# Four stage borders of a transformer, spectral and scan kernel: where SBUF tiles lie and when first loads are queued

## Chip, cores and metric

One Trainium2 chip, one of its cores. The metric is device time in microseconds of one execution; lower is better. The kernel has five instruction streams that matter here: PE (matmul), VectorE (DVE), ScalarE (ACT), GpSimd (POOL) and SyncE (SP), which issues nearly all DMAs. Each stream runs its instructions in order.

## What is computed

The input is one image of 48 x 48 tokens with 768 channels, in f32. Four layers follow one another:

```
# layer 0: transformer block, 12 heads of 64
qkv  = layernorm(x) @ qkv_w + qkv_b
attn = softmax(q @ k.T * scale + rel_h[...] + rel_w[...])     # 2304 x 2304 per head
x    = x + (attn @ v) @ proj_w + proj_b
x    = x + gelu(layernorm(x) @ w1 + b1) @ w2 + b2             # 768 -> 3072 -> 768
# layers 1 and 3: spectral mixing
xs   = rfft2(x)                                               # complex, over the 48 x 48 grid
o1   = relu(block_diag(xs, w1) + b1); o2 = block_diag(o1, w2) + b2   # 8 blocks of 96, complex
x    = irfft2(softshrink(o2, 0.01)) + x
# layer 2: twelve steps of a 3 x 3 depthwise diffusion with gates, then silu(H @ W_out + b_out)
```

## The kernel before

The kernel is one straight program; its stages come one after the other and meet at five borders.

**Queries, keys, values** (`qkv_phase`). Tokens are handled in three superblocks `sb` of 768. For each, matmuls make q, k, v (dense products run as seven products of half blocks instead of eight; the sums of weight blocks that this needs are made once and stored). Beside them run 24 "position steps" per superblock: 12 of `rel_h` and 12 of `rel_w` (L400). A step loads a table `relD` of 192 KB (L378, four buffers), runs four matmuls, and its result is split by ACT and VectorE into three bf16 parts (L370 to L373), which go to DRAM as `rh_d` and `rw_d` (L389). `advance()` (L433) issues loads until three steps are ready, then runs one step. At the end of the last superblock 16 steps are left. A bound on the scores is computed (L460 to L477), four steps run (L478), the work pools are closed, `ahead(1)` (L481, `load_ahead`, L1283) opens the attention's tiles and issues nine loads for its first chunk (one of queries, L516; eight of biases, L495 and L496), and then the remaining twelve `rel_w` steps run.

**Attention.** A branch on the bound picks `attention_bounded` (the one that runs here) or `attention_any`. 36 chunks (6 pairs of heads x 6 query blocks of 384) have six work items each; in an item PE runs `products` (L556), `scores` (L564) and the `values` of the item before (L585). Beside it POOL makes the block sums of the projection and MLP weights (`weight_sums`), the projection's into `ps_d`.

**Projection** (`proj_phase`). After the branch, all seven blocks of `ps_d` are loaded (L714), 576 KB each. `block_sums` adds parts of oT on VectorE (L136 to L139). Blocks n=0 and n=1 use oT itself as left operand, n=2 the first sum. A block is nine matmuls, which the trace lists as 18 entries.

**MLP** (`mlp_phase`). Twelve hidden tiles per half (`ml_h`), weights in four slots (`ml_w`), seven products of the second layer per superblock (`product`, L911); each product has twelve steps f of three matmuls, six entries in the trace. Between them `follow` (L1507) takes the first transform of the next layer along: a call runs the rows loaded by the call before (L1353, result stored to `yu`, L1355), and loads the next input from `xa_d` (L1499), the MLP's stored output. In the very last product the calls are at f=3 and f=9:

```
                    if f in ((3, 9) if (sb, n) == (NTB // 2 - 1, 6) else (6,)):
                        follow(psum)
```

The last block of half 0 comes after the MLP, in steps 1 and 4 of the mix.

**First spectral layer** (`afno_first`, `spectrum_mix`). Per item (40 of them, in 44 pipelined steps): f_x (L1412), block products (L1426 to L1428, L1447, L1448), f_u (L1462); input tiles `yt` are read from `yu` (L1385), four items each, and results `us` stored back (L1469). Then the rows are gathered again (`gt`, L1483) for the last transform f_w (L1549), whose result is x2T, the scan's input. The same mix runs for layer 3 (`afno_second`), where f_w (L1580) is followed by an addition on VectorE (L1582) and the output's DMAs.

**Scan** (`scan_phase`). Its input projection is L1076, its twelve steps L1166, its output L1228 and L1237.

**What sets the order and the waits.** SBUF pools are stacks, one from the left and one from the right. A pool waits until all tiles of the pools whose place it takes are done with. The order of the instructions of an engine is made by the framework's scheduler: first in code goes first, but where an instruction's inputs are not ready yet by the scheduler's own reckoning, a later one that is ready goes ahead. [...]

The places that matter at the border from MLP to spectrum, in bytes per partition: ml_c (constants, x2nT and sums) 17,056 to 52,544; ml_x 52,544 to 71,716; ml_w 71,744 to 96,320; x1 (rows of `follow`) 96,320 to 121,344; ml_h 129,504 to 229,344. Over them: f1_g (gathers and rows) 17,056 to 48,608; f1_c (spectral weights, o1) 48,608 to 76,512; f1_y (yt, us) 76,512 to 114,912; f1_s 114,912 to 134,112. So f1_c and f1_y reach into ml_w.

Of the kernel before, what the change touches and what calls it, by code (L numbers as in the profile page):

```python
# [11 lines left out]
F32 = mybir.dt.float32  # L12
# [7 lines left out]
P = 128  # L20
G = 48
T = G * G
# [6 lines left out]
TB = 384  # L29
NTB = T // TB  # L30
# [6 lines left out]
NB, BS = 8, 96  # L37
# [142 lines left out]
def qkv_phase(tc, ident, x, qkv_w, qkv_b, relT, rel_d, ln_g, ln_b, q_d, k_d, v_d, rw_d, rh_d, wqk_d, wv_d, flag, home, ahead):  # L180
# [18 lines left out]
    with (  # L199
# [163 lines left out]
        with tc.tile_pool(name="qkv_o", bufs=1, side="right") as op:  # L363
# [114 lines left out]
            for _ in range(4):  # L478
                advance()
            inner.close()  # L480
            ahead(1)  # L481
            while steps or ready:
                advance()
# [36 lines left out]
    return keys_values, chunk  # L520


def attention_bounded(tc, ahead, oT, beside):

# [14 lines left out]
    with (  # L539
# [64 lines left out]
        for i in range(len(work) + 1):  # L604
            if i % 7 == 3:
                next(other, None)
            if i < len(work):
                c, k0 = work[i]
                pr, qc = c
                if k0 == 0:  # L610
                    nxt = (pr, qc + 1) if qc + 1 < T // QB else (pr + 1, 0)
                    if nxt[0] < NC:
                        load_chunk(qbs[nxt[1] % 2], nxt)
                    if qc == 1 and pr + 1 < NC:
                        load_keys_values(kvs[(pr + 1) % 2], pr + 1)
# [13 lines left out]
            pass  # L629


def attention_any(tc, ident, oneh, q_d, k_d, v_d, rw_d, rh_d, oT, beside):


    nc = tc.nc
# [2 lines left out]
    with tc.tile_pool(name="an_o", bufs=2) as op:  # L638
        for _ in beside(op, lambda name: op.tile([P, 2, TB], F32, tag="p", name=name)):
            pass  # L640
    with (
        tc.tile_pool(name="an_c", bufs=1) as cp,
        tc.tile_pool(name="an_h", bufs=1) as hp,
# [11 lines left out]
        for h in range(NH):  # L655
# [5 lines left out]
            for i in range(NTB):  # L661
                load_bias(nc, bt[:, :, :, i * TB : (i + 1) * TB], rw_d, rh_d, h, i)
            for t in range(NT):
                s = sp.tile([P, T], F32, tag="s", name=f"an_s_{h}_{t}")
# [12 lines left out]
                nc.scalar.activation(s, s, AF.Exp, bias=nm)  # L677
                if t % GQ == 0:
                    pT = pp.tile([P, NT, GQ * P], F32, tag="pT", name=f"an_pT_{h}_{t}")
                col = (t % GQ) * P  # L680
                for k0 in range(0, NT, 4):
                    n = min(4, NT - k0)
                    ps = ps_t.tile([P, 512], F32, tag="t", name=f"an_pt_{h}_{t}_{k0}")
                    for j in range(n):
                        k = k0 + j
                        nc.tensor.transpose(ps[:, j * P : (j + 1) * P], s[:, k * P : (k + 1) * P], ident)
                    ev(pT[:, k0 : k0 + n, col : col + P], ps[:, : n * P].rearrange("p (k q) -> p k q", q=P))
                if t % GQ == GQ - 1:
# [12 lines left out]


def proj_phase(tc, x, ps_d, proj_b, oT, xr_d):

    nc = tc.nc
    with (
# [2 lines left out]
        tc.tile_pool(name="pj_x", bufs=1, side="right") as xp,  # L709
        tc.tile_pool(name="pj_p", bufs=6, space=PSUM) as pm,  # L710
    ):
        w = wp.tile([P, 7, NC2, TB], F32, tag="w", name="pj_wt")
        for n in range(7):
            nc.sync.dma_start(w[:, n], ps_d[:, n])  # L714
        pb = load_bcast(nc, wp, proj_b, C, "pj_b")
        for sb in range(NTB // 2):
            rows = lambda n: slice((2 * sb + n) * TB, (2 * sb + n + 1) * TB)
# [11 lines left out]
                nc.gpsimd.tensor_tensor(o, o, added[half, n], ALU.add)  # L729
                nc.sync.dma_start(xr_d[rows(n), cols(half)].rearrange("(t p) c -> p t c", p=P), o)  # L730

            rows_in_seven(nc, pm, f"pj_{sb}", rhs, lambda n: w[:, n], xp, emit)


def weight_sums(nc, pool, gate, pw, w1, w2, ps_d, w1s_d, w2s_d):
# [51 lines left out]
def mlp_phase(tc, ident, w1s_d, b1, w2, w2s_d, b2, ln_g, ln_b, xr_d, xa_d, follow_in):  # L787
# [8 lines left out]
    with (  # L796
# [91 lines left out]
        def second_layer(sb):  # L888
# [22 lines left out]
            def product(n, left, right):  # L911

                ps = [pm.tile([P, 512], F32, tag="m", name=f"p2_{sb}_{n}_{t}") for t in range(3)]
                for f in range(NF2):
# [12 lines left out]
                        V.tensor_tensor(hs[1, f], hs[1, f], hs[2, f], ALU.subtract)  # L927
                        V.tensor_tensor(hs[0, f], hs[3, f], hs[2, f], ALU.subtract)

                    if f in ((3, 9) if (sb, n) == (NTB // 2 - 1, 6) else (6,)):  # L930
                        follow(psum)
                return [p[:, :TB] for p in ps]

# [323 lines left out]
def block_kernel(ctx: ExitStack, tc: tile.TileContext, a: dict):  # L1257
# [48 lines left out]
    w2s_d = dram.tile([4, P, NF2, TB], F32, tag="w2s_d", name="w2s_d")  # L1306
    ps_d = dram.tile([P, 7, NC2, TB], F32, tag="ps_d", name="ps_d")
    beside = lambda pool, gate: weight_sums(nc, pool, gate, a["proj_w"], a["mlp_w1"], a["mlp_w2"], ps_d, w1s_d, w2s_d)
    bounded = nc.values_load(flag)
    with tc.If(bounded > 0) as which:  # L1310
        attention_bounded(tc, ahead, oT, beside)
    with which.Else():
        attention_any(tc, ident, oneh, q_d, k_d, v_d, rw_d, rh_d, oT, beside)
    at_stack.close()
    xr_d = dram.tile([T, C], F32, tag="xr_d", name="xr_d")
    proj_phase(tc, x, ps_d, a["proj_b"], oT, xr_d)
    oT_close()
    xa_d = dram.tile([NTB, TB, C], F32, tag="xa_d", name="xa_d")
    yu = [dram.tile([YR, G // 2, TB], F32, tag=f"yu{i}", name=f"yu{i}") for i in range(2)]
# [6 lines left out]
    nc.sync.dma_start(wsc, a["W_scan"].rearrange("(c p) n -> p c n", p=P))  # L1326
    afno_first(tc, a, yu, x2T, follow_in)

    closes = []

# [27 lines left out]
def spectrum_mix(tc, name, a, layer, yu, psum, keep, side, halves, beside):  # L1358
# [9 lines left out]
    HB = NB // 2  # L1368
    with (
        tc.tile_pool(name=f"{name}_c", bufs=1, side=side) as cp,  # L1370
        tc.tile_pool(name=f"{name}_y", bufs=2, side=side) as yp,
        tc.tile_pool(name=f"{name}_s", bufs=2, side=side) as sp,
    ):
        fh = cp.tile([BS, BS], F32, tag="fh", name=f"{name}_fh")
# [6 lines left out]
        ys = {}  # L1381

        def load(half, kc):
            yt = yp.tile([BS, KC, TB], F32, tag="yt", name=f"{name}_yt_{half}_{kc}", bufs=3)
            nc.sync.dma_start(yt, yu[half][4 * KC * kc : 4 * KC * (kc + 1)].rearrange("(k q) p c -> (q p) k c", q=4))  # L1385
            us = yp.tile([BS, KC, TB], F32, tag="us", name=f"{name}_us_{half}_{kc}")
            ys[half, kc] = yt, us

        nc.sync.dma_start(w1t, w1)
# [6 lines left out]

        o1s = []
        for i in range(3):
            o1 = cp.tile([BS + 1, KC, 3, G], F32, tag=f"o1{i}", name=f"{name}_o1{i}")
            nc.vector.memset(o1[BS : BS + 1, :, :, :], 0.0)  # L1400
            nc.vector.memset(o1[BS : BS + 1, :, 1, :], 1.0)
            o1s.append(o1)
# [75 lines left out]
            beside(step)  # L1478


def load_spectrum(nc, pool, yu, half, g, name):
    gt = pool.tile([YR, 4, TB], F32, tag="gt", name=f"{name}_gt_{half}_{g}", bufs=3)
    nc.sync.dma_start(gt, yu[half][:, 4 * g : 4 * g + 4, :])  # L1483
    return gt

# [32 lines left out]
    return follow  # L1518


def afno_first(tc, a, yu, x2T, follow_in):

# [6 lines left out]
    x2v = x2T.rearrange("p c (h w) -> p c h w", w=HD)  # L1529
    nc.gpsimd.memset(x2v[:, :, :, G:], 0.0)  # L1530
    with (
        tc.tile_pool(name="f1_g", bufs=1, side="left") as gp,
        tc.tile_pool(name="f1_p", bufs=8, space=PSUM) as pm,
    ):

# [2 lines left out]

        iw = gp.tile([4 * KW, BS], F32, tag="iw", name="f1_iw")
        follow = follow_in(gp, 1)  # L1540
        spectrum_mix(tc, "f1", a, "L1", yu, psum, True, "left", (1, 0), lambda step: follow(psum) if step in (1, 4) else None)
        nc.sync.dma_start(iw, a["iw"])
        for half in (1, 0):
            for g in range(NTB):
                gt = load_spectrum(nc, gp, yu, half, g, "f1")
# [7 lines left out]
def afno_second(tc, a, x3, yu):  # L1553
# [4 lines left out]
    with (  # L1558
# [15 lines left out]
        for half in range(2):  # L1574
            cols = slice(half * TB, (half + 1) * TB)
            for g in range(NTB):
                gt = load_spectrum(nc, gp, yu, half, g, "f3")
                for i in range(4):
                    ps = psum(f"w_{half}_{g}_{i}")
                    nc.tensor.matmul(ps[:BS, :TB], lhsT=iw, rhs=gt[: 4 * KW, i, :], start=True, stop=True)  # L1580
# [118 lines left out]
```

## Time and profile before

| | |
|---|---|
| three timed runs | 3902.34, 3902.94, 3906.36 us (median 3902.94) |
| the profiled execution | 3896.0 us |
| its span, first to last instruction | 3893.8 us |
| PE busy | 3755.5 us, 96% |
| VectorE, ACT, POOL busy | 53%, 29%, 17% |
| mean granted PE clock | 0.977 |
| bytes moved | 460.43 MB, mean 118 GB/s |
| chain that ended last | PE 87%, DVE 5%, DMA 4% |

The stages on the span's clock, by their first matmuls: queries, keys and values to 480, the last position steps to 510, attention 513.5 to 1690.1, projection from 1701.2, MLP from about 1838 to 2854.2, first mix from 2872.5, f_w from about 3070, scan projection from 3133.7, scan from 3296.8, second mix 3655.3 to 3849.1, last stage to the end.

How to read it: a row of the time order gives start, length, engine, source line, operation and tiles, a count, and in brackets the idle time before it with what ended it. A row of the waits gives who waited for what, the sum, how many times and the longest. "SPq" is the queue of DMA issues, where a length covers a run of several. A row of the windows gives the busy time of PE, PE's weight loads, DVE, ACT and POOL with counts, then the granted PE clock, the DMA engines' busy share and GB/s.

### The profile page before, as it was taken

The page shows a single profiled execution, that of the slowest core. Times are in us where ns is not written, and L with a number is a line of the kernel's source. Part 1 is how long each engine was busy: PE and PEld are TensorE (multiplying, and loading weights), DVE is VectorE, ACT ScalarE, POOL GpSimd, SP SyncE. Part 2 cuts the span into 40 slices and gives each one's busy share as a digit, 9 for nine tenths or more (in the row PEclk, how much of TensorE's full clock was granted, in tenths as well). Part 3 has the DMA queues.
Part 4 walks back from the last instruction along what each step waited for, and adds up shares of the span by engine and source line. Part 5 has one row for each costly group of instructions (what it writes and reads, how often), then busy time and mean ns, then how long its engine had stood idle before and what let it go on. Part 6 is the DMA issues. An engine that isn't in the chain of part 4 may idle for free.

```text
span 3893.8 us, 54463 instructions
## 1 busy us (share of the span) xinstructions
PE 3755.5 (96%) x22018; PEld 2283.2 (59%) x22018; DVE 2050.0 (53%) x3185; ACT 1141.6 (29%) x1907; POOL 654.2 (17%) x496
## 2 busy tenths in 40 slices
PE   8999989999999999989999999999979998999998
PEld 4666544444444444445555555555558876996685
DVE  6655456666666666545425233232335358995445
ACT  1322244444444444411310120021013246223341
POOL 3101011111111111024000000000023210981131
PEclk9999999999999999999999999999989789999999
DMA  7656563424232322134335434533443312110434
GB/s 256 212 186 199 177 182 95 132 88 131 96 98 89 98 89 73 30 114 161 118 106 161 151 102 123 155 111 109 142 116 98 95 36 96 35 37 23 145 98 167
DMA packets 266954, 460.43 MB, mean 118 GB/s; under 512 B 33005, under 2 KB 219365, under 8 KB 260327
## 3 DMA queue, kind: packets, MB, share of 16 engines
q1 hardware_dynamic: 257063, 436.23, 36.4%
q10 hardware_dynamic: 9632, 20.65, 1.4%
q8 instruction: 175, 2.87, 0.3%
q14 instruction: 84, 0.69, 0.1%
HBM read 318.49 MB, written 138.31 MB: 117 GB/s over the span
## 4 chain that ended last, share of the span: by engine, by line
PE 87%; DVE 5%; DMA 4%; ACT 2%; issue 1%; SPq 1%; POOL 1%; ACTq 0%; DVEq 0%; POOLq 0%
PE p L860 13%; PE p L923 13%; PE s L556 11%; PE av L585 11%; PE qk L294 6%; PE s L564 6%; PE c L1076 4%; PE v L163 3%; PE pj L163 2%; PE f_z L1447 2%; PE f_z L1448 2%; PE f_x L1412 2%; PE f_u L1462 2%; PE so L1237 2%; PE f_w L1549 2%; DVE s L1186 2%
## 5 line engine op out<-in xcount | busy, mean ns | idle before, releaser
L574 DVE TENSOR_TENSOR acc<-acc,p 128x768 f32<-128x768 f32 x576 | 581.8, 1010 | 354.1 <-ACT p L566 315.9
L566 ACT ACTIVATE p<-s 128x768 f32<-128x768 f32 x648 | 478.4, 811 | 688.7 <-PE s L564 578.9
L923 PE MATMUL p<-w,h 128*128 128x384 f32 x1512 | 492.7, 486 | 0.0
L556 PE MATMUL s<-qt,kv 64*128 64x384 f32 x2592 | 477.7, 501 | 8.4 <-ACT p L566 4.7
L585 PE MATMUL av<-p,kv 128*64 128x384 f32 x2592 | 464.5, 493 | 0.0
L923 PEld LDWEIGHTS p<-w,h 128*128 128x128 f32 x1512 | 286.3, 190 | 196.7
L556 PEld LDWEIGHTS s<-qt,kv 64*128 64x128 f32 x2592 | 232.7, 186 | 248.8 <-ACT p L566 113.8
L585 PEld LDWEIGHTS av<-p,kv 128*64 128x64 f32 x2592 | 170.0, 136 | 225.2 <-issue 215.9
L860 PE MATMUL p<-x2nT,w 128*128 128x384 f32 x864 | 293.2, 489 | 3.9 <-POOL rr L899 3.9
L294 PE MATMUL qk<-xnT,wqk 128*128 128x384 f32 x756 | 251.5, 489 | 5.6 <-DMA wqk<-wqk_d 5.6
L1166 PE MATMUL c<-H,bands 128*48 128x96 f32 x5632 | 242.1, 247 | 11.7 <-issue 11.5
L564 PE MATMUL s<-bt,oneh 120*128 120x384 bf16 x1296 | 248.8, 328 | 0.0
L1166 PEld LDWEIGHTS c<-H,bands 128*48 128x48 f32 x5632 | 234.1, 123 | 19.8 <-issue 11.9
L860 PEld LDWEIGHTS p<-x2nT,w 128*128 128x128 f32 x864 | 165.2, 191 | 119.4 <-POOL rr L899 4.1
L860 PE MATMUL p<-xT,w 128*128 128x384 f32 x648 | 220.8, 486 | 0.0
L564 PEld LDWEIGHTS <-oneh 120*128 120x128 bf16 x1296 | 109.3, 98 | 174.5 <-issue 115.4
L294 PEld LDWEIGHTS qk<-xnT,wqk 128*128 128x128 f32 x756 | 144.2, 192 | 99.7 <-issue 7.9
L899 POOL TENSOR_TENSOR rr<-rr,ml_b 128x1152 f32<-128x1152 f32 x12 | 32.1, 2675 | 955.0 <-DMA rr<-xr_d 861.6
L855 ACT ACTIVATE h<-h,ml_b 128x384 f32<-128x384 f32 x144 | 88.3, 614 | 345.9 <-DVE h L875 174.3
L1174 POOL TENSOR_TENSOR t<-s,c 128x768 f32<-128x768 f32 x80 | 144.7, 1835 | 171.9 <-DVE s L1136 160.8
L860 PEld LDWEIGHTS p<-xT,w 128*128 128x128 f32 x648 | 123.2, 190 | 85.8
L1076 PE MATMUL c<-wsc,x2T 128*112 128x357 f32 (+1 forms) x576 | 151.6, 426 | 2.0 <-DVE c L1037 2.0
(312 smaller groups left out, 4763.5 us busy)
## 6 DMA issues: line engine op xcount, KB each, us to landing
w<-w1s_d SPq DMA_DIRECT2D x36, 768.0 KB
w<-w2s_d SPq DMA_DIRECT2D x36, 768.0 KB
bt<-rh_d SPq DMA_DIRECT2D x144, 162.0 KB
w<-w1s_d SPq DMA_DIRECT2D x36, 576.0 KB
w<-in_mlp_w_dram SPq DMA_DIRECT2D x27, 768.0 KB
wqk<-wqk_d SPq DMA_DIRECT2D x12, 1344.0 KB
yu<-f_ys SPq DMA_DIRECT2D x24, 672.0 KB
f_gt<-yu SPq DMA_DIRECT2D x24, 672.0 KB
```

The lines of the kernel that those rows point to most:

```text
L163: nc.tensor.matmul(p[:, :TB], lhsT=rhs[n][:, c, t * P : (t + 1) * P], rhs=w[:, c, :], start=c == 0, stop=c == NC2 - 1)
L294: nc.tensor.matmul(p[:, :TB], lhsT=w[:, n, c, :], rhs=ops[sb][n][:, c, :], start=c == 0, stop=c == NC2 - 1)
L556: nc.tensor.matmul(ps[:, s, :QB], lhsT=keys[pr % 2][rows, kt * P : (kt + 1) * P], rhs=qbs[qc % 2][0][rows], start=True, stop=False)
L564: nc.tensor.matmul(ps[:, s, :QB], lhsT=oneh[:NBR, b % 3, :], rhs=qbs[qc % 2][1][:NBR, s, b // 3, j, :], start=False, stop=True)
L566: nc.scalar.activation(p, ps[:, :, :QB], AF.Exp)
L574: nc.vector.tensor_tensor(probs[c], probs[c], p, ALU.add)
L585: nc.tensor.matmul(avs[c][rows, :QB], lhsT=vals[pr % 2][:, kt, rows], rhs=p[:, s, :], start=kt == 0, stop=kt == NT - 1)
L860: nc.tensor.matmul(p[:, :TB], lhsT=w[n][:, c, :], rhs=rhs[n][:, c, :], start=c == 0, stop=c == NC2 - 1)
L923: nc.tensor.matmul(ps[t][:, :TB], lhsT=hs[left, f][:, t * P : (t + 1) * P], rhs=wt[:, f % KW2, :], start=f == 0, stop=f == NF2 - 1)
L1076: nc.tensor.matmul(ps[:K, i, :n], lhsT=xT[:, cc, tok : tok + K], rhs=w[:, cc, c0 : c0 + n], start=cc == 0, stop=cc == NC - 1)
L1166: nc.tensor.matmul(ps[r0 : r0 + G, k // 4, cols], lhsT=bands[:, n - GC, i, :] if gr else bands0[:, n, i, :], rhs=H[:, n, :, d : d + NPR], ...
L1174: GP.tensor_tensor(t, sc[:, ch], c1[:, m0 : m0 + GC].unsqueeze(2).to_broadcast([P, GC, RR, NPR]), ALU.mult)
```

## The change

The diff has five parts.

1. Five more position steps are issued before `ahead(1)`, so ahead of the first chunk's loads in code.
2. A tile `pw` for the first two of the seven projection blocks is allocated beside oT, and loaded by one DMA inside both branches of the attention (eight items before the end in the one that runs). `proj_phase` loads five blocks. In `attention_any` one buffer less is used, to make room.
3. The spectral pools are laid out anew. f1_g goes to the right side; the three o1 tiles and `us` go from f_c and f_y to f_s. By the sizes in the code the first mix's pools then lie at 17,056 to 36,320 (f1_c), 36,320 to 59,360 (f1_y), 59,360 to 102,560 (f1_s) and 109,344 to 140,896 (f1_g, below x2T and wsc). The calls of `follow` in the last product go from f=3 and 9 to 2 and 6.
4. The scan's weights wsc are loaded at step 8 of the first mix instead of ahead of it.
5. In the last stage `gt` has four buffers instead of three. In layer 3, f3_c, f3_y and f3_s then lie at 54,752 to 74,016, to 97,056 and to 140,256.

```diff
@@ qkv_phase
             for _ in range(4):
                 advance()
             inner.close()
+            for _ in range(5):
+                advance()
             ahead(1)
@@ attention_bounded (and attention_any: load_next() after the weight sums, s with bufs=1)
             if i % 7 == 3:
                 next(other, None)
+            if i == len(work) - 8:
+                load_next()
@@ proj_phase(tc, x, pw, ps_d, proj_b, oT, xr_d)
-        w = wp.tile([P, 7, NC2, TB], F32, tag="w", name="pj_wt")
-        for n in range(7):
-            nc.sync.dma_start(w[:, n], ps_d[:, n])
+        w = wp.tile([P, 5, NC2, TB], F32, tag="w", name="pj_wt")
+        for n in range(5):
+            nc.sync.dma_start(w[:, n], ps_d[:, 2 + n])
-            rows_in_seven(nc, pm, f"pj_{sb}", rhs, lambda n: w[:, n], xp, emit)
+            rows_in_seven(nc, pm, f"pj_{sb}", rhs, lambda n: w[:, n - 2] if n > 1 else pw[:, n], xp, emit)
@@ mlp_phase, product
-                    if f in ((3, 9) if (sb, n) == (NTB // 2 - 1, 6) else (6,)):
+                    if f in ((2, 6) if (sb, n) == (NTB // 2 - 1, 6) else (6,)):
@@ block_kernel
+    pw, pw_close = opened("pw", [P, 2, NC2, TB], "right")
+    load_pw = lambda: nc.sync.dma_start(pw, ps_d[:, :2])
-    proj_phase(tc, x, ps_d, a["proj_b"], oT, xr_d)
+    proj_phase(tc, x, pw, ps_d, a["proj_b"], oT, xr_d)
+    pw_close()
-    nc.sync.dma_start(wsc, a["W_scan"].rearrange("(c p) n -> p c n", p=P))
-    afno_first(tc, a, yu, x2T, follow_in)
+    afno_first(tc, a, yu, x2T, follow_in, lambda: nc.sync.dma_start(wsc, a["W_scan"].rearrange("(c p) n -> p c n", p=P)))
@@ spectrum_mix
-        tc.tile_pool(name=f"{name}_y", bufs=2, side=side) as yp,
+        tc.tile_pool(name=f"{name}_y", bufs=3, side=side) as yp,
-            yt = yp.tile([BS, KC, TB], F32, tag="yt", name=f"{name}_yt_{half}_{kc}", bufs=3)
+            yt = yp.tile([BS, KC, TB], F32, tag="yt", name=f"{name}_yt_{half}_{kc}")
-            us = yp.tile([BS, KC, TB], F32, tag="us", name=f"{name}_us_{half}_{kc}")
+            us = sp.tile([BS, KC, TB], F32, tag="us", name=f"{name}_us_{half}_{kc}")
-            o1 = cp.tile([BS + 1, KC, 3, G], F32, tag=f"o1{i}", name=f"{name}_o1{i}")
+            o1 = sp.tile([BS + 1, KC, 3, G], F32, tag=f"o1{i}", name=f"{name}_o1{i}", bufs=1)
@@ load_spectrum: gt with bufs=bufs; 3 in afno_first, 4 in afno_second
@@ afno_first
-        tc.tile_pool(name="f1_g", bufs=1, side="left") as gp,
+        tc.tile_pool(name="f1_g", bufs=1, side="right") as gp,
-        spectrum_mix(tc, "f1", a, "L1", yu, psum, True, "left", (1, 0), lambda step: follow(psum) if step in (1, 4) else None)
+        spectrum_mix(tc, "f1", a, "L1", yu, psum, True, "left", (1, 0), lambda step: follow(psum) if step in (1, 4) else load_next() if step == 8 else None)
```

More of the change, by code (lines that the diff above doesn't have):

```diff
@@ L520, in attention_loads, with attention_bounded @@
     return keys_values, chunk
-def attention_bounded(tc, ahead, oT, beside):
+def attention_bounded(tc, ahead, oT, beside, load_next):
     nc = tc.nc
@@ L629, in attention_bounded, with attention_any @@
             pass
-def attention_any(tc, ident, oneh, q_d, k_d, v_d, rw_d, rh_d, oT, beside):
+def attention_any(tc, ident, oneh, q_d, k_d, v_d, rw_d, rh_d, oT, beside, load_next):
     nc = tc.nc
@@ L640, in attention_any @@
             pass
+    load_next()
     with (
@@ L663, in attention_any @@
             for t in range(NT):
-                s = sp.tile([P, T], F32, tag="s", name=f"an_s_{h}_{t}")
+                s = sp.tile([P, T], F32, tag="s", name=f"an_s_{h}_{t}", bufs=1)
                 m6 = sp.tile([P, T // TB], F32, tag="m6", name=f"an_m_{h}_{t}")
@@ L700, in attention_any, with proj_phase @@
                     nc.vector.tensor_tensor(oT[r0 : r0 + HD, h // 2, g * n : (g + 1) * n], avs, bc[:HD, :n], ALU.mult)
-def proj_phase(tc, x, ps_d, proj_b, oT, xr_d):
+def proj_phase(tc, x, pw, ps_d, proj_b, oT, xr_d):
     nc = tc.nc
@@ L1308, in block_kernel @@
     beside = lambda pool, gate: weight_sums(nc, pool, gate, a["proj_w"], a["mlp_w1"], a["mlp_w2"], ps_d, w1s_d, w2s_d)
+    pw, pw_close = opened("pw", [P, 2, NC2, TB], "right")
+    load_pw = lambda: nc.sync.dma_start(pw, ps_d[:, :2])
     bounded = nc.values_load(flag)
     with tc.If(bounded > 0) as which:
-        attention_bounded(tc, ahead, oT, beside)
+        attention_bounded(tc, ahead, oT, beside, load_pw)
     with which.Else():
-        attention_any(tc, ident, oneh, q_d, k_d, v_d, rw_d, rh_d, oT, beside)
+        attention_any(tc, ident, oneh, q_d, k_d, v_d, rw_d, rh_d, oT, beside, load_pw)
     at_stack.close()
     xr_d = dram.tile([T, C], F32, tag="xr_d", name="xr_d")
-    proj_phase(tc, x, ps_d, a["proj_b"], oT, xr_d)
+    proj_phase(tc, x, pw, ps_d, a["proj_b"], oT, xr_d)
+    pw_close()
     oT_close()
@@ L1478, in spectrum_mix, with load_spectrum @@
             beside(step)
-def load_spectrum(nc, pool, yu, half, g, name):
-    gt = pool.tile([YR, 4, TB], F32, tag="gt", name=f"{name}_gt_{half}_{g}", bufs=3)
+def load_spectrum(nc, pool, yu, half, g, name, bufs):
+    gt = pool.tile([YR, 4, TB], F32, tag="gt", name=f"{name}_gt_{half}_{g}", bufs=bufs)
     nc.sync.dma_start(gt, yu[half][:, 4 * g : 4 * g + 4, :])
@@ L1518, in afno_follow, with afno_first @@
     return follow
-def afno_first(tc, a, yu, x2T, follow_in):
+def afno_first(tc, a, yu, x2T, follow_in, load_next):
     nc = tc.nc
@@ L1544, in afno_first @@
             for g in range(NTB):
-                gt = load_spectrum(nc, gp, yu, half, g, "f1")
+                gt = load_spectrum(nc, gp, yu, half, g, "f1", 3)
                 for ct in range(NC // 2):
@@ L1576, in afno_second @@
             for g in range(NTB):
-                gt = load_spectrum(nc, gp, yu, half, g, "f3")
+                gt = load_spectrum(nc, gp, yu, half, g, "f3", 4)
                 for i in range(4):
```

## The prediction

> **What bounds the kernel now.** I read the page first: PE is busy 96% of the span and carries 87% of the chain that ended last, so only time in which PE stands still, or runs at a lower clock, can be won. The list of PE's waits over the whole span says where it stands still (columns: sum in us, times, longest):
>
> ```profile
> PE f_x L1412 <- DMA f_yt<-yu: 18.2, 1, 18.2
> PE pj L163 <- DMA pj_wt<-ps_d: 11.2, 1, 11.2
> PE rw L400 <- DMA relD_w<-in_relD_dram: 11.0, 3, 9.7
> PE f_w L1580 <- DMA f_gt<-yu: 5.2, 5, 1.3
> ```
>
> All entries of the list together are some 130 us; these four, 46 us, are at the places that the diff touches, and all four wait for a DMA. The largest of the others (first LayerNorm 17.7, start of the scan 11.5) are not touched. Next I read SP's queue and PE's work at each of the four. Before the attention, SP's queue in order of time:
>
> ```profile
> 484.28 1.74 SPq L378 DMA_DIRECT2D relD_w<-in_relD_dram  x2
> 486.80 0.33 SPq L516 DMA_DIRECT2D qt<-q_d  x1
> ...
> 492.28 1.21 SPq L389 DMA_DIRECT2D rh_d<-rh  x2
> 493.53 2.28 SPq L496 DMA_DIRECT2D bt<-rh_d  x1
> 495.91 10.47 SPq L378 DMA_DIRECT2D relD_w<-in_relD_dram  x10
> ```
>
> The last ten position tables stand behind the first queries and biases (L516, L495, L496). At the spectrum, PE, then SP (two answers):
>
> ```profile
> 2850.85 3.39 PE L923 MATMUL p<-w,h 128*128 128x384 f32 x10
> 2872.47 1.89 PE L1412 MATMUL f_x<-f_fh,f_yt 96*96 96x96 f32 x10 [18.23 <-DMA f_yt<-yu]
> ```
> ```profile
> 2837.30 14.69 SPq L1355 DMA_DIRECT2D yu<-f_ys  x2
> 2854.27 0.32 SPq L1375 DMA_DIRECT2D f_fh<-in_fh_dram  x1
> ...
> 2860.86 0.39 SPq L1326 DMA_DIRECT2D wsc<-in_W_scan_dram  x1
> ...
> 2862.10 0.43 SPq L1385 DMA_DIRECT2D f_yt<-yu  x1
> ```
>
> The MLP's last product ends at 2854.24 and the next load goes at 2854.27: the spectral pools wait for a place of the MLP's weights. fh, w1, w2 and the 1839 KB of wsc then go ahead of yt, which lands at 2872.4. And after the attention PE's last `av` ends at 1690.08:
>
> ```profile
> 1688.62 1.46 PE L585 MATMUL av<-p,kv 128*64 128x384 f32 x6
> 1701.24 14.07 PE L163 MATMUL pj<-pj_wt,oT 128*128 128x384 f32 x36 [11.16 <-DMA pj_wt<-ps_d]
> ```
>
> **1. Position tables before the first queries.** Nothing is added; five table loads (L378) get priority over nine loads of the first chunk on SP. The queue isn't in code order (iw, coded after the mix, went at 2816.8), so they will interleave. Today PE runs two `rw` steps by 489.83, waits 9.70, and ends the twelfth at 509.86; VectorE ends the last split at 514.5 (L373), having had nothing from 494.0 to 501.64. Its pace is 1.12 us a step (rest_w starts 509.43, 510.55, 511.67). With tables always there it would go on at 494.0: 10 x 1.12 + 0.6 = 11.8, end 506, gain 8.4. The DMA engines don't allow quite that: they are 0.6 to 0.97 busy from 486 to 500, and the bytes (10 tables of 192 KB, chunk 1.3 MB, rh store 0.9 MB) at some 230 GB/s take 18 us from 486.8, so 505, and VectorE ends near 507.5: gain 7. If the biases still slip in front, 0. I take 6. Late next: the first chunk's biases, issued perhaps 6 us later, landing near 502 to 505, when the attention starts near 507.5; if all nine went after the five tables (5 x 1.1 us) they would land near 507 to 510 and take back up to 3. Below zero is excluded short of that, since the same DMAs are issued.
>
> **2. First two blocks of projection weights inside the attention.** One DMA more on SP in the attention (1152 KB), two fewer of 576 KB after it. The attention's SP has slack (the last chunk's loads go by 1621, and its first use is six items of 5.3 us before 1690, at 1658) and its DMA slices are 0.1 to 0.4 busy, so I cost it at nothing; without that cover, some 4 us. After the attention PE needs pw (there), oT of the last chunk (L600, ends 1692.07), and its own jump over the other branch. No row shows PE's jump alone; VectorE's is near: L600 ends at 1692.07 and L136 starts at 1695.55, with its inputs long there: 3.48 us. [...] by the row it starts at 1690.08 + 3.5 = 1693.6 and gains 7.6. I take the row, and 0.4 more for the clock: PEclk is 0.5 until about 1706 today, which costs 2.4 us, and a gap of 3.64 us before the attention still cost 1.6 (12 `s` matmuls took 3.29 instead of 2.21, and so on). So 8, from 6 to 10. Next late: block n=2, issued at about 1695.0 and landed some 6 us later, as today's first; PE needs it after 12.3 us (36 x 0.3225, plus the clock), near 1706. Its left operand (L138) ends at 1699.6. Covered by 5 us.
>
> **3. Spectral tiles over places that are free.** The constants' pool now lies at 17,056 to 36,320 bytes, over ml_c only; yt at 36,320 to 59,360, over ml_c and ml_x. Their last reader is POOL's L899 near 2815 (fw and iw, under such places, went at 2816.4 and 2816.8). So fh, w1, w2, ih and POOL's w1s, w1d (1.80 us each) go into product 5, where POOL is idle, behind nobody that PE needs before 2845 (the weights of product 6). Then yt waits for yu alone. The last rows move from f=9 to f=6: 3 x 6 x 0.3225 = 5.8 us, so the store goes at 2851.66 - 5.8 = 2845.9; the store before it (2837.30) had left the DMA engines by 2840.5, so 2849. Its input (L1499, 2830.30) was down by 2836, the row is due at 2841.6. A yt of 720 KB then takes 4 to 5 us (f_x, 576 KB, took about 5): 2853.5. VectorE empties the last banks at 2855.1 (the store of the last block goes at 2855.11). So PE starts at 2855.2 instead of 2872.47: 17.3. The start-up from the first f_x to the first f_u took 17.5 today at half clock; the same stretch in the second mix, after a gap of 1.87, took 3670.81 - 3655.34 = 15.5: another 2.0. Against it: POOL's memset of x2T (L1530, 3.9 us) waits for the last MLP store (landed 2860.8) and can stand before an Xs or an o1 sign: 0 to 1, I take 0.8. Sum 18.5. [...] But the second mix fell to half after gaps of 1.4 to 1.9, so I take the row. wsc moves behind yt; it is needed at 3133. f1's gather buffers on the other side delay the scan's bias loads until 3131.7; they need 3 to 4 us and VectorE needs them 6 us later. Nothing. The other attention branch doesn't run.
>
> **4. Fourth gather buffer in the last stage.** From 3855 to 3890 the DMA share is at its top:
>
> ```profile
> 3865.00:3870.00 5.00, 4.03 (x13) 1.84 (x13) 3.20 (x7) 0.00 (x0) 0.00 (x0) 1.00 1.06 390
> 3875.00:3880.00 5.00, 3.74 (x12) 1.79 (x12) 2.84 (x6) 0.00 (x0) 0.00 (x0) 1.00 1.04 377
> ```
>
> So the stage is bound by bytes (last two columns: DMA share, GB/s) and not by PE's 5.2 us of waits. One gather of 672 KB moves to about 3765, where DMAs are idle: 0.69 MB / 380 GB/s = 1.8 us, from 0 to 2.5.
>
> **Sum.** 6 + 8 + 18.5 + 1.8 = 34.3, some 34. The profiled execution took 3896.0 (span 3893.8 and 2.2 around it), so its like would be 3862. The median of the three timed runs, 3902.94, lies 6.9 higher; from it 3902.9 - 34 = 3869. The terms' bounds give 21 to 41, that is 3862 to 3882.
>
> **Rivals.**
> *The spectral wait changes hands* (chance 0.17). fw now lies over the MLP's hidden tiles and waits for the last store, 2860.8. If SP's order has it, or that store, before yt, yt goes at 2861 and lands at 2865.5; or the memset comes before the first Xs, which then ends near 2865.4. Either way part 3 gives 9 instead of 18.5: 3878. For it: SP and POOL are in order, and today's POOL had the memset before Xs. Against: yt and Xs are ready some us before the store is down.
> *The first queries become what is late* (0.07): part 1 gives 2 or 3, 3872.
> *The waits are not removed* (0.03): the scheduler puts the loads where they were; 3895 to 3903.
> *Slower* (0.03): the clock. In f_w (3071 to 3139) PE is 10.00 busy of 10 us at PEclk 0.50, so steady work of small matmuls doesn't always bring the clock back. If the first mix, now entered with short gaps, stayed at half, a step of 4.57 us would take about 1.9 times that (z pairs start 0.32 apart at half, 0.17 at full): 4.1 us lost a step, so from 11 of the 44 steps on the whole gain and the bound of 8 us are gone; 20 steps give 3951. Against: both mixes recovered within 27 us.
>
> **Numbers.** The likeliest case has 0.70. 0.2% (8 us) is about what a measurement of this kernel can tell from no change. Faster 0.94, within 0.03, slower 0.03. The range goes from the bound of the likeliest, with 2 us for the spread of the runs, to the far side of the first rival: 3860 to 3886.
>
> **What would show it.** Part 1: PE's wait for relD_w below 3, the first `s` near 507, no wait of `s` for bt. Part 2: PE's gap after the last `av` 2 to 4 us, the next wait of pj for pj_wt none. Part 3: fh and w1 issued near 2817 (in the old time), yt before the last xa_d store, the gap at f_x under 2. Part 4: four gathers near 3765, the last stage 1 to 2 us shorter. It is wrong if f_x still waits 8 or more, or if the scan, the attention or f_w change in length.

## The result and the profile after

| | before | after |
|---|---|---|
| median of the timed runs, us | 3903.28 | 3877.39 |
| range of the timed runs | 3902.34 to 3906.36 (4) | 3876.30 to 3878.67 (4) |
| ratio after/before | | 0.9932, 95% interval 0.9915 to 0.9950 |
| profiled execution, us | 3896.0 | 3878.45 |
| span of the profile, us | 3893.8 | 3876.6 |
| mean granted PE clock | 0.977 | 0.978 |

The medians differ by 25.9 us, the two profiled executions by only 17.5. Which of the two the change is worth is a question of its own; the experiment b_again answers it. The forecast was a gain of 34. Single executions of one kernel spread with the granted clock: of 36 of the kernel before, three took 3880 to 3883 us at a mean clock of 0.981 or 0.982, the others 3896 to 3910 at 0.972 to 0.977.

The parts are numbered here as in the prediction: the loading of the scan's weights (4 in the list of the change) counts with part 3, and part 4 is the fourth gather buffer.

First the list of PE's waits of the changed kernel (columns: sum in us, times, longest):

```profile
PE f_o L1434 <- POOL f_Xs L1424: 9.2, 4, 4.9
PE s L558 <- ACT p L568: 7.4, 2, 5.7
...
PE f_w L1588 <- DMA f_gt<-yu: 6.0, 3, 4.7
PE rw L400 <- DMA relD_w<-in_relD_dram: 5.6, 2, 5.2
...
PE f_x L1420 <- issue: 3.7, 1, 3.7
...
PE pj L163 <- DVE pj_u L168: 2.1, 1, 2.1
...
PE pj L163 <- issue: 1.5, 1, 1.5
PE f_x L1420 <- DMA f_yt<-yu: 1.4, 1, 1.4
PE pj L163 <- DVE ln_q L80: 1.3, 1, 1.3
```

The wait of 18.2 for `yt` is now 1.4, the one of 11.2 for `pj_wt` is gone (1.5 is left, for nothing that the profile names). The one for `relD_w` has gone from 11.0 to 5.6 in this list, but only half of that fall is real: at the same matmuls PE now waits 2.67 for VectorE's `rw` (the row that follows), and four other kernels with part 1 show 8.4 to 8.8 for `relD_w` and no such wait. Other rows have come or grown: `f_o` waits for POOL's `Xs` 4.9 at a stretch (1.5 before), `s` for ACT's `p` 5.7 (3.2), `pj` for VectorE's `pj_u` and `ln_q` (none), `f_w` of the last stage for one gather 4.7 (1.3), and `f_x` at the start of the second mix 3.7 for nothing that the profile names (1.9 for ACT). So waits have come up beside those that went; the experiments show which of them a part caused.

```profile
496.16 3.75 PE L400 MATMUL rw<-q,relD_w 128*96 128x96 f32 x24 [2.67 <-DVE rw L373]
```

The three borders. SP's queue before the attention:

```profile
485.92 4.54 SPq L378 DMA_DIRECT2D relD_w<-in_relD_dram  x4
...
491.98 0.83 SPq L378 DMA_DIRECT2D relD_w<-in_relD_dram  x2
...
496.56 1.61 SPq L497 DMA_DIRECT2D bt<-rw_d  x1
...
500.26 6.75 SPq L378 DMA_DIRECT2D relD_w<-in_relD_dram  x5
```

Seven tables now stand before or among the biases; the last five still stand behind them. The last table's issue ends 26.4 us after the last `qk` (480.62), where before it was 27.3 (506.38, against 479.07): the end of the queue has hardly moved. PE after the attention, then PE and SP at the spectrum (three answers):

```profile
1690.60 1.46 PE L587 MATMUL av<-p,kv 128*64 128x384 f32 x6
1693.57 11.88 PE L163 MATMUL pj<-pw,oT 128*128 128x384 f32 x36 [1.51 <-issue]
```
```profile
2850.69 1.06 PE L1420 MATMUL f_x<-f_fh,f_yt 96*96 96x96 f32 x10 [1.39 <-DMA f_yt<-yu]
...
2860.41 1.11 PE L1434 MATMUL f_o<-f_Xs,f_w 96*96 96x240 f32 x2 [4.90 <-POOL f_Xs L1424]
```
```profile
2812.30 0.34 SPq L1383 DMA_DIRECT2D f_fh<-in_fh_dram  x1
...
2844.76 0.85 SPq L1393 DMA_DIRECT2D f_yt<-yu  x2
2849.93 0.38 SPq L914 DMA_DIRECT2D xa_d<-rr  x1
```

fh goes 37 us before the MLP's end instead of at it, and `yt` ahead of the last store, as forecast. After the attention the first 36 entries take 11.88 (14.07 before): no half clock is left there.

To see what each part is worth, I cut the span at the first or last matmul of each stage. The lengths, in us, for all twelve profiles, those of the experiments below included ("without" are the profiles of kernels in which the part is not made, "with" those in which it is, leaving out the ones that edit that stretch further; how many is in brackets):

| stretch (part) | without | with |
|---|---|---|
| last `qk` to first `s` (1) | 34.2 to 34.8, mean 34.5 (5) | 31.8 to 32.4, mean 32.1 (5) |
| last `qk` to last `av` (1) | 1211.0 to 1214.4, mean 1213.0 (5) | 1210.8 to 1211.4, mean 1211.2 (4) |
| last `av` to first `pj` (2) | 10.6 to 11.2, mean 10.8 (3) | 1.2 to 1.8, mean 1.4 (9) |
| first `pj` to first transposition (2) | 124.5 to 125.2, mean 124.9 (3) | 126.2 to 127.3, mean 126.7 (7) |
| last `av` to the MLP's end (2) | 1164.2 to 1165.2, mean 1164.7 (3) | 1154.5 to 1157.2, mean 1156.1 (7) |
| MLP's end to first `f_x` (3) | 18.2 to 19.2, mean 18.7 (3) | 1.0 to 1.4, mean 1.2 (7) |
| first `f_x` to first `f_u` (3) | 17.3 to 18.4, mean 17.7 (3) | 17.5 to 18.0, mean 17.9 (7) |
| first `f_w` of the last stage to the end (4) | 44.7 to 51.4, median 46.3 (5) | 45.4 to 46.2, mean 45.7 (7) |

So part 1 gives 1.8 by the attention's end (less sure than the 2.3 at the first `s`, as the profiles without it spread over 3.4 there), part 2 gives 8.6, part 3 gives 17.4, part 4 between nothing and 1: 28 to 29, where the medians have 25.9 with an interval of about 19 to 33. The longer wait of `f_x` at the second mix is in no row: from the first matmul of the scan's projection to that `f_x` it takes 521.8 on average with part 3 (nine profiles, 519.7 to 524.8) and 521.7 without (three).

### The profile page after: what moved, and what is told of

The parts are those of the page before. It is cut to its first block, busy times and chain, and to the rows that moved or that the text cites. A ratio compares the mean times of both kernels' runs of the same rounds, so it can differ in the third digit from the quotient of the medians.

```text
span 3876.6 us, 54460 instructions
## 1 busy us (share of the span) xinstructions
PE 3761.5 (97%) x22018; PEld 2285.7 (59%) x22018; DVE 2059.0 (53%) x3185; ACT 1141.9 (29%) x1907; POOL 658.4 (17%) x496
```

## Experiments

Times of the kernel before, over all the comparisons with it, go from 3880 to 3909.5 us, so I read nothing out of a difference of 3 us in two medians alone; the stretches above are sharper. All experiments are of the changed kernel with an edit unless said otherwise.

### The changed kernel without part 1

```diff
             inner.close()
-            for _ in range(5):
-                advance()
             ahead(1)
```

> The changed kernel without part 1: the five extra advance() are taken out, so the first queries and biases again go ahead of the position tables. By my present theory, from the trace of the changed kernel, part 1 gives nothing: the first `s` came 0.7 us earlier (2.2 counted from the end of the last qk), but the wait of `s` for ACT's p near 550 grew from 3.2 to 5.7 us and the attention ended 2.0 us later on the clock. So without it the attention ends 0 to 2 us earlier than in the changed kernel and the time is 3875 to 3877. By the prediction part 1 gives 6, so 3883. A third possibility is that the growth of the wait near 550 comes from part 2's pool and not from part 1; then the wait stays at 5.7 here, PE's waits for relD_w go back to 11, and the time is some 2 us above the changed kernel, 3879.

Measured: 3879.66 us (3873.69 to 3881.07). From the last `qk` to the first `s` 34.6, to the last `av` 1212.8, against 32.2 and 1211.4 in the changed kernel; PE's waits for `relD_w` are back at 11.7. So my theory that part 1 gives nothing falls, by the first `s`: the later end of the attention in the profiled pair (1692.06 against 1690.08) came from an earlier stage that happened to be 1.6 us later and from an attention that was short in the one execution of before. The prediction's 6 falls too. It is 2.3 at the first `s`, and 1.8 at the attention's end.

### The kernel before with part 2 alone

```diff
-        w = wp.tile([P, 7, NC2, TB], F32, tag="w", name="pj_wt")
+        w = wp.tile([P, 5, NC2, TB], F32, tag="w", name="pj_wt")
...
+            if i == len(work) - 8:
+                load_next()
```

> The kernel before with part 2 alone: two blocks of the projection's weights loaded in the attention. By the prediction 8 us, so 3895. By my present theory PE starts the projection some 9.6 us earlier against the end of the attention, a gap of 1.5 instead of 11.2, but the residual (x loaded, added on POOL, stored, loaded again for the second LayerNorm) starts no earlier, and VectorE's LayerNorm stands ahead of the evacuation of the projection's PSUM: waits of 2.1, 1.3 and 0.9 us for pj_u, ln_q and pj_o come back, so the gain at the MLP's first matmul is 5 to 6 and the time 3897 to 3898. The times hardly tell 3895 from 3898; the three waits in the trace do.

Measured: 3894.69 us, ratio 0.9981 (0.9973 to 0.9989), 8.5 us less. The gap after the attention is 1.3, and the waits are back at the same place of the list:

```profile
PE pj L163 <- DVE pj_u L168: 1.7, 1, 1.7
...
PE pj L163 <- DVE ln_q L80: 1.3, 1, 1.3
```

The mechanism is as expected, the net larger than I thought. By the means of the table it is 9.4 less in the gap, 1.8 more to the first transposition (waits of some 4, and 2.2 of half clock saved), and 1.0 less from there to the MLP's end. The time of this kernel holds two other differences that part 2 doesn't explain: in its profile f_w is 6.9 shorter and the last stage some 5 longer than in the others.

### The kernel before with part 3 alone

```diff
-            us = yp.tile([BS, KC, TB], F32, tag="us", ...)
+            us = sp.tile([BS, KC, TB], F32, tag="us", ...)
-            o1 = cp.tile([BS + 1, KC, 3, G], F32, ...)
+            o1 = sp.tile([BS + 1, KC, 3, G], F32, ..., bufs=1)
...
-        tc.tile_pool(name="f1_g", bufs=1, side="left") as gp,
+        tc.tile_pool(name="f1_g", bufs=1, side="right") as gp,
...
```

The loading of wsc at step 8 and the calls of `follow` at f=2 and 6 are in it too.

> The kernel before with part 3 alone: the spectral tiles' layout, wsc's load and the order of the last rows. By the prediction 18.5, so 3884.5. By my present theory, from the changed kernel's trace, 16.8 from the gap before the first f_x, nothing from the start-up of the mix (POOL's memset of x2T again stands before the second Xs, some 5 us of PE's wait for it), and 2 to 3 lost at the second mix, where a gap of 3.7 leaves PE at half clock for longer: 13.5 to 16.5 in all, 3886.5 to 3889.5. By the first rival 9, so 3894.

Measured: 3887.84 us, ratio 0.9966 (0.9951 to 0.9980), 15.4 us less. The gap before `f_x` is 1.0, the start-up 18.0 with a wait of 4.8 for `Xs`. How the gain divides between the layout, wsc and the earlier rows is not tested, as all three change here together. My extra loss at the second mix is not there: `f_x` waits 3.8 at its start, as expected, but from its first `f_x` to the last stage it takes 196.5, against 196.1 in a second profile of the kernel before; it is the first profile, with 193.7, that is short.

### The kernel before, profiled once more

No edit.

> The kernel before, unchanged, profiled once more. Its profiled execution took 3896.0, 7 below the median of its timed runs, while the changed kernel's profiled execution lies 1 above its median: so the two profiles differ by 17.5 where the medians differ by 25.9. If executions of the kernel before vary in one wait, a second profile near 3903 shows which (the waits for a DMA at the three borders are the first to look at: 18.2, 11.2 and 9.7). If it comes out at 3896 again, the difference lies between profiled and timed executions, and no trace can show it.

Measured: 3901.76 us, span 3900.0. Against the first profile the attention is 2.4 longer (1178.9 and 1176.6, while eight other kernels with the same attention loop have 1178.0 to 1179.6), the second mix 2.4, the projection and the MLP 1.0. None of the waits at the three borders differs by more than 0.6. So the pair of profiles shows 17.5 because the one execution of before was a short one in stages that the change doesn't touch; the medians and the stretches are what to go by.

### Weight sums later in the attention

```diff
-            if i % 7 == 3:
+            if i % 7 == 3 and i > 3:
                 next(other, None)
```

> The changed kernel, with the weight sums beside the attention begun at group 10 of the key tiles instead of group 3. My theory of part 1: its 2.3 us at the first `s` are taken back near 550, where ACT's p waits for a place that the first weight sum (pw0b) holds until POOL has read it; that load goes only when the store of rw is out, which the change doesn't make earlier. With the sums begun later no p waits there: the wait of `s` for ACT's p near 550 (5.7 in the changed kernel) goes, and the attention, from the first `s` to the last `av`, takes 1172 to 1174 instead of 1178.2 to 1179.6; the time is 3 to 6 below the changed kernel, 3872 to 3874. If the places of p aren't what holds it (the biases of the second chunk, say), the wait stays and the time too, 3877.

Measured: 3869.10 us, ratio 0.9912 (0.9899 to 0.9926). The attention takes 1171.4. ACT in the changed kernel, then in this one, at the same item (two answers):

```profile
549.35 2.21 ACT L568 ACTIVATE p<-s 128x768 f32<-128x768 f32 x3 [10.60 <-POOL pw0p L130]
```
```profile
540.29 2.21 ACT L568 ACTIVATE p<-s 128x768 f32<-128x768 f32 x3 [3.09 <-PE s L566]
545.59 2.22 ACT L568 ACTIVATE p<-s 128x768 f32<-128x768 f32 x3 [3.09 <-PE s L566]
```

The first weight sum holds a place in the ring of `p` (the row names POOL's `pw0p`) until its block has been loaded. By SP's queue that load (541.5) stands behind the second chunk's biases, which stand behind the store of `rw` (513.8). With the sums begun later the stall is gone, and with it the half clock that followed it (12 entries of `s` took 4.21, now 2.21): 7.8 us together. The stall is in the kernel before as well (3.2 to 5.9 in five kernels without part 1). Part 1 doesn't cause it; it only ends there in part: counted from the last `qk`, PE resumes at 69.4 to 70.2 with part 1 and at 70.8 to 72.4 without.

### The zeros of x2T in pieces

```diff
-    nc.gpsimd.memset(x2v[:, :, :, G:], 0.0)
...
                     ev(x2v[:, half * NC // 2 + ct, 8 * g : 8 * g + 8, :G], ...)
+                    if half:
+                        for c in (ct, NC // 2 + ct):
+                            nc.gpsimd.tensor_scalar(x2v[:, c, 8 * g : 8 * g + 8, G:], x2v[:, NC // 2 + ct, 8 * g : 8 * g + 8, : HD - G], 0.0, None, ALU.mult)
```

> The changed kernel, with the zeros of x2T written in 36 small pieces beside the emptying of f_w's banks (POOL, zero times a part of x2T) instead of by one memset of 3.9 us ahead of the second Xs. The theory: the memset waits for the last store of the MLP and then runs 3.94, with the second Xs behind it on POOL, and PE's longest wait for Xs (4.9; 4.8 and 3.8 in two other runs of this layout) is that. Without it this wait is 1.4 as in the second mix, the stretch from the first f_x to the first f_u takes 14 to 15.5 instead of 18.0, and the time is 3 to 4 lower, 3873.5. If Xs waits for something else there, X of ACT or a bank, the stretch stays at 18.

Measured: 3869.80 us, ratio 0.9911 (0.9898 to 0.9925). POOL in the changed kernel, and PE here (two answers):

```profile
2852.47 0.68 POOL L1424 TENSOR_TENSOR f_Xs<-f_X 96x240 f32<-96x240 f32 x1 [31.04 <-ACT f_X L1422]
2854.99 3.94 POOL L1538 MEMSET x2T<- 128x4608 f32 x1 [1.84 <-issue]
2858.89 0.81 POOL L1445 TENSOR_SCALAR f_o<-f_o 96x240 f32<-96x240 f32 x1
2859.67 0.68 POOL L1424 TENSOR_TENSOR f_Xs<-f_X 96x240 f32<-96x240 f32 x1
```
```profile
2852.36 1.81 PE L1420 MATMUL f_x<-f_fh,f_yt 96*96 96x96 f32 x10
2855.64 1.11 PE L1434 MATMUL f_o<-f_Xs,f_w 96*96 96x240 f32 x2 [1.48 <-POOL f_Xs L1424]
```

The memset did stand between the two `Xs`, and the wait falls from 4.9 to 1.5 without it. But the start-up falls by 1.7 only, to 16.3, not to 14 or 15.5: PE is at half clock for some 10 us here (ten `f_x` in 1.81, at full 1.06), until after the third group of `f_x`, against some 7 us in the changed kernel, so what the wait gives back the slower clock takes in part. It needn't: a_all, with the same edit here, takes 14.9, as its half clock lasts some 7 us:

```profile
2840.90 1.53 PE L1425 MATMUL f_x<-f_fh,f_yt 96*96 96x96 f32 x10
```

So the memset costs 1.7 to 3.1, and what sets the length of the half clock is open. The median is lower by 7.6. The rest is not explained by the edit: the profile has 2.4 of it in the scan and its transform, where a_no5 without this edit is as short, and 1.8 between the attention and the MLP's end.

### The residual's x ahead of the projection's last weights

```diff
-        for n in range(5):
-            nc.sync.dma_start(w[:, n], ps_d[:, 2 + n])
+        load_w((0, 1))
         pb = load_bcast(nc, wp, proj_b, C, "pj_b")
...
             for half, n in ((0, 0), (0, 1), (1, 1), (1, 0)):
+                if sb == 0 and half and n:
+                    load_w((2, 3, 4))
```

> The changed kernel, with the first three loads of x in the projection put ahead of its weight blocks 4 to 6 (behind blocks 2 and 3, which PE needs first). The theory: after part 2 the residual is what is late, since its x still lands behind five blocks of weights: POOL's first add starts at 1713.41 in the changed kernel and at 1713.22 in the kernel before; stores and the second LayerNorm follow from it, and VectorE's LayerNorm stands ahead of the emptying of the projection's banks (waits of 2.1, 1.3 and 0.9 of pj for pj_u, ln_q and pj_o). With x some 5 us earlier the three waits are below 1 together, and from the first pj to the first transposition it takes 123 instead of 127: 3873.5. The rival: the LayerNorm comes earlier too, but stands at the same place of VectorE's order, and PE waits as long as before, so 3877, or longer if block 4 lands late.

Measured: 3875.45 us (3870.80 to 3877.92). POOL's first additions of x in the changed kernel and here (two answers):

```profile
1713.41 2.62 POOL L731 TENSOR_TENSOR pj_x<-pj_x,pj_b 128x1152 f32<-128x1152 f32 x1 [191.94 <-DMA pj_x<-in_x_dram]
...
1718.69 11.13 POOL L731 TENSOR_TENSOR pj_x<-pj_x,pj_b 128x1152 f32<-128x1152 f32 x3
```
```profile
1706.09 2.63 POOL L736 TENSOR_TENSOR pj_x<-pj_x,pj_b 128x1152 f32<-128x1152 f32 x1 [186.04 <-DMA pj_x<-in_x_dram]
```

x comes 7 us earlier (6 counted from the last `av`), the wait for `pj_u` is gone, but those for `ln_q` (1.6) and `pj_o` (0.9) stay: from the first `pj` to the first transposition 125.4, not 123. Both theories hold half. The residual is what delays the LayerNorm, and the LayerNorm's place in VectorE's order still costs 2.5.

### More position tables first

```diff
-            for _ in range(5):
+            for _ in range(12):
                 advance()
```

> The changed kernel with twelve extra advance() instead of five: eleven of the twelve position tables stand ahead of five of the first chunk's nine loads. The theory of part 1's small gain: five of the twelve tables still stood behind bias loads, from 500.26, and PE waited 5.2 for the ninth or so; the DMA engines were at 0.93 to 0.96 of their time from 492 to 504, so this is bytes and not order alone. With all tables early PE's waits for relD_w fall to 1 or 2 and the first `s` waits for bias instead, at about the same place: from the last qk to the first `s` 30 to 32.5 (32.2 in the changed kernel, 34.2 to 34.8 without part 1). By the record's reckoning it would be 28 to 29. In the time nothing that can be told: 3876 to 3878.

Measured: 3874.64 us (3872.97 to 3876.38). SP's queue here:

```profile
494.22 5.63 SPq L378 DMA_DIRECT2D relD_w<-in_relD_dram  x4
499.91 0.39 SPq L498 DMA_DIRECT2D bt<-rh_d  x1
...
502.09 0.35 SPq L378 DMA_DIRECT2D relD_w<-in_relD_dram  x1
```

From the last `qk` to the first `s` 29.4, less than my 30 to 32.5 and near the record's 28 to 29, and no `s` waits for a bias. So the bytes were not the limit that I had now thought: the order was, and the last table's issue ends 22.7 us after the last `qk`. With eleven tables ahead of the last five biases part 1 is worth 5.1 at the first `s`; with seven, 2.3.

### Three gather buffers in the last stage

```diff
-                gt = load_spectrum(nc, gp, yu, half, g, "f3", 4)
+                gt = load_spectrum(nc, gp, yu, half, g, "f3", 3)
```

> The changed kernel without part 4: three gather buffers in the last stage. From the first f_w of the last stage to the end of the span it took 45.5 to 46.1 us in six kernels with four buffers, and 44.7, 45.1 and 46.3 in three with three (51.4 in a fourth). The theory: the stage is bound by bytes, and the gather fetched early only lets the output stores, which share the DMA engines, come later: the same 45 to 46, the time 3877 as in the changed kernel. By the prediction it is 1.8 longer here, 47.4 and 3879.

Measured: 3878.62 us (3877.18 to 3883.13); the last stage and its stores 46.8. That lies between the two expectations, 1.1 above the changed kernel's 45.7 on average, inside the 44.7 to 51.4 of the kernels with three buffers. A row of the changed kernel's windows, near the end, shows the DMA share (last but one) above 1:

```profile
3856.00:3861.00 5.00, 4.03 (x13) 1.75 (x12) 3.13 (x6) 0.00 (x0) 0.00 (x0) 1.00 1.05 402
```

The fourth gather went early, at 3747, as forecast, and the stage stays bound by bytes (the share is 1.02 to 1.05 in each window from 3841 to 3866). Whether part 4 is worth 1 or nothing can't be told apart here.

### All four edits together

> The changed kernel with the four edits of the last round together: twelve advance() instead of five, weight sums from group 10 on, the first x ahead of the projection's weights 4 to 6, the zeros of x2T in pieces. If each takes away a wait of its own, the stretches add up: 29.4 from the last qk to the first `s`, 1171.4 for the attention, 125.4 from the first pj to the first transposition, 16.3 from the first f_x to the first f_u; against the changed kernel 2.8 + 7.9 + 2 + 1.7 = 14.4, so 3863. If they are late for one another (the biases of the second chunk once the first `s` is 5 us earlier, for one), a wait of `s` appears between 509 and 550 and the sum is 3 to 5 short, 3866 to 3868.

Measured: 3861.94 us (3833.61 to 3868.04; the lowest is one execution, at a mean granted clock of 0.987, of which there is no trace), ratio to before 0.9878 (0.9854 to 0.9902); 15.5 below the changed kernel. The stretches add up: 29.8 to the first `s`, 1172.8 for the attention, 123.8 for the projection, 14.9 for the mix's start-up. No wait of `s` takes their place. The profiled execution took 3867.8. In it the first mix after its start-up and f_w together are 2.3 longer than in the changed kernel, and so they are, by 2.1 and 2.3, in a_no5 and a_gt3, and from the scan's projection to the second mix it takes 2.8 longer; the cause of these stays open.

## Why the prediction was right, and where its terms were not

The time is inside the range, 8 above the likeliest 3869, and the mechanisms of the likeliest case are those that ran: each of the three large waits fell. The sum was 6 to 8 too large, and the terms stand like this.

**Part 1: 6 forecast, 1.8 measured.** The step that failed is "I take 6" between 0 ("if the biases still slip in front") and 8.4, and of the signs that it named, `relD_w` waited 5.2 instead of below 3 and the first `s` came at 512.8 instead of 507. SP's queue did interleave, as the text said, and five tables were left behind five bias loads: the last one went only 0.9 us earlier, counted from the last `qk`, and the chain ends with the last one. a_adv12 has 5.1 of the 6, with eleven tables in front of the last biases; the reckoning of pace and bytes, which gave 7, was near for such a queue, but the estimate gave nearly its whole gain to an edit that moves only part of the queue. The forecast "late next" (biases) never came: `s` waits for no bias in any of the runs. So the second rival, with 2 or 3 for part 1, had the size but not the reason. What came was the stall near 550, which stood in the profile of before as the longer wait of `s` for `p` and which part 1 partly runs into.

**Part 2: 8 forecast, 8.6 measured, by errors that cancel.** It is luck in part: the gap gave 9.4 (7.6 forecast), the clock 2.2 (0.4 forecast), and waits of some 4 that were put at nothing went off. The text took VectorE's restart of 3.48 after the branch as the measure of PE's. PE stood 1.2 to 1.8 in nine kernels; VectorE stood 3.44 again in the changed kernel. The row of before names the landing of an MLP load as what ended the 3.48, so whether it shows a restart at all is not settled:

```profile
1695.55 1.36 DVE L136 TENSOR_TENSOR pj_xT<-oT 128x1152 f32<-128x1152 f32 x1 [3.48 <-DMA ml_b<-in_mlp_b_dram]
```

Either way a row of another engine was a poor measure here: PE's gap is 1.7 to 2.3 shorter than the 3.5 taken from it. Nor did PE need the last part of oT first: it started at 1693.57, while VectorE wrote that part until 1694.03. What was not seen is the residual: its x load stood behind the weights before and after (POOL's first addition at 1713.22 and 1713.41), so once PE began 8 us earlier the second LayerNorm and the emptying of banks behind it were late. b_pw shows the waits without the other parts, a_pjx that an earlier x takes one of them away. The step "covered by 5 us" was right for the weights and asked about nothing else.

**Part 3: 18.5 forecast, 17.4 measured.** The gap gave 17.6 (17.3 forecast), by early constants and `yt` ahead of the last store. The term that was off is the start-up: 2.0 gained less 0.8 for the memset, measured 0. Most of the memset's length reached PE (a wait of 4.9 instead of 1.5), and a_zero shows that even without it half clock remains. Without the memset the stretch takes 14.9 to 16.3, around the forecast's 15.5; the size that was off is above all the memset's, 1.7 to 3.1 instead of 0.8. In a_zero PE fell to half (ten `f_x` in 1.81 instead of 1.06) with gaps of 1.44 and 1.45, the only ones in the 13 us before it. The text had expected half clock to remain after gaps of that size, rightly, but the second mix's 15.5, from which it took the size, was 16.3 to 18.3 in each of the eleven other profiles.

**Part 4: 1.8 forecast, 0 to 1 measured.** The bytes that moved, over the rate of the busiest windows, came to more than the move was worth here; why is not shown.

**The first rival** named the measured time, 3878, but not for its reason: it put part 3 at 9, with `yt` or the first `Xs` late. `yt` went before the last store; the memset came after the first `Xs`, not before it. Its memset half was real, at 1.7 to 3.1 instead of 9.5. The slower case, half clock through the first mix, did not come: after about 2865 it ran at full clock.

## What to carry to other kernels

When a wait of an engine is removed, follow every chain that starts at the same border, not only the operand that was late: here the residual and a ring of buffers lent to side work were next, and the list of waits named neither as such. Where a queue interleaves by readiness, look at which loads remain behind after the edit, and cost only those that moved. To size parts of a few us, cut the spans of several kernels at the same matmuls and compare stretches; two single profiles differed by 6 us in stages that nobody had touched.

## What the runs showed of the hardware that was not expected

In the changed kernel VectorE's L136, L137 and L138 (additions of two parts of SBUF tiles) took 2.38, 3.65 and 3.31 us, while POOL's three additions beside them took 11.13; apart, in the kernel before, VectorE's took 1.35, 1.36 and 1.35 (from 1727.43 on) and POOL's three 7.78 (1718.70 to 1726.48). Together the six ran from 1717.56 to 1729.82, 12.3 us, and one after the other they would take 11.8: side by side these six took no less time. Why is not shown.

The f_w stage stays at half clock for its whole 61 us with PE busy in every microsecond in eleven of the twelve profiles (0.50 granted and PE 10.00 of 10 in the windows of the kernel before, the changed one and a_all; the row of f_w takes 60.7 to 61.6 us in ten of the eleven). In b_pw its first 10 us ran at 1.00, and the stage was 6.9 us shorter (56.3 instead of 63.1). Steady work alone doesn't bring the clock back here, and what decides is open.
